# Small reorderings in a four-layer convolution and attention kernel: the samples and the end of layer 0, one weight sum of the MLP, and five places in layers 1 to 3

## The chip, the cores and the metric

The kernel runs on one core of a Trainium2 chip. The metric is the device time in microseconds (us) of one execution, lower is better. The profile comes from one execution, and its times count from the first instruction of that execution.

## What is computed

The reference applies four layers, one after the other, to x of shape (2, 512, 32, 32), that is two batches of 512 channels and 1024 pixels. All values are float32.

```python
# layer 0: attention with sampled keys and a learned bias over positions
q = gconv1x1(bn(x), qw)                        # 8 groups of 64 channels
off = tanh(pw @ gelu(dwconv6x6_stride4(q)))*4  # 64 offsets for each group
kv = grid_sample(bn(x), grid + off)            # bilinear samples
k, v = gconv1x1(kv, kw), gconv1x1(kv, vw)
pos = grid_q - grid_kv                         # 1024 x 64 pairs for each group
bias = relu(relu(sign(pos)*log1p(|pos|) @ w1 + b1) @ w2 + b2) @ w3 + b3
x = x + out_w @ softmax(q k / 8 + bias) v + out_b
x = x + w2 @ gelu(w1 @ bn(x) + b1) + b2        # the MLP, 512 -> 2048 -> 512
# layer 1: group norm, 8-head attention, projection, residual
# layer 2: group norm, 1-head attention, projection, residual
# layer 3: q, k of 64 channels, softmax over axis 1, gamma * (v attn) + x
```

## The kernel before

**Layer 0.** The two batches and four pairs of groups make eight units, t = 0 to 7. A loop over i = 0 to 255 works on 32 steps for each unit. In every step `second` (L623) makes four bias tiles: the matmuls of L630 fill a two-bank PSUM tile z, and ACT evicts it with a Relu (L639). Tiles z come from a pool of three PSUM tiles, and everything else in layer 0 that needs PSUM (`zt`) takes its tile from the same pool. DVE makes the inputs (L613) and joins the four results in two steps (L644). The rest of the unit's work is a chain of generators, `behind`: `finish(t)`, then `offsets(t + 2)`, then `samples(t + 1)`. After every second z tile, one `next(behind)` runs the chain to its next `yield`, and what it emits stands behind that z tile in each engine's queue. Such a place is called a slot here: eight slots make four steps. At the first and the third tile of each step with i % 4 == 1, `scale_tab` (L601) puts one more activation of 128x512 on ACT. Counted from the first slot of a step with i % 4 == 0 as slot 0, these two stand in the gaps after slots 1 and 2 of every eight.

`samples(t)` broadcasts two coordinates into a PSUM tile `gpb` (L504), then makes `near` for two axes with two activations each (L512, L513) in one slot. In the following slots it makes `wx` and the eight planes of `wy` from `gpb` (L519, L520, L523; two planes in the first slot, then three and three), a Relu over all of `wy` (L526), and then the products and copies of keys and values.

Joined tiles are added up over partitions by DMAs with an add, which POOL's queue issues (L970 and its neighbours). The sum of step i - 1 is added to it at step i by L970. For the last step it is a DVE add (L988). The result is summed by `third` (L659) into PSUM tile `sim`, of two banks, and `scores` (L667) adds the query-key product.

`finish_last` (L731) ends the last unit. For each half of 512 columns it issues `third`, `scores` and an ACT copy into `simb` (L743). Then come eight transposes (L753), the row maxima (L754), 16 exponentials with their sums (L761), a division (L770), transposes back (L775), a copy (L776) and the output projection (L719), which DVE adds to x (L729). The pieces `project_out(pps[0], b, 0, [2])` and `project_out(pps[1], b, 1, range(2))` don't depend on the softmax. They stand between the two sets of transposes.

**MLP.** Products use seven multiplications for a 2x2 block product (Strassen's way with sums of Winograd). In block 0, `form2` makes sums of the second weight on DVE: four adds of 128x1024 (L161) for each half of the columns. One add is taken for each chunk c from 4 on by L1353, and the rest after the loop. DVE also forms `upper` (L1306 to L1309) and the right-hand sums of `hid` (L173 to L176).

**Layers 1 to 3.** Every engine keeps the order that the program writes. Eight PSUM banks rotate under one tag. `group` (L1463) does a seven-product group: with K of two chunks its order is x0, y5, v4, z3, x1, y6, v2. Product y6 accumulates on y, so it waits until DVE has read y for u2 (L1494). DVE then makes u3 (L1506), and `evict` combines the rest. Small work stands in tracks with written costs and waits, and `do_chores` takes from them three times in each group, and twice in each turn of `attend`.

- `group_norm` (L1212) yields between its parts. `over_group` multiplies by a matrix of group means (L1224), yields, and then copies the PSUM result on DVE (L1227). Four Newton turns (L1247 to L1249) follow with no yield between.
- `divide` (L1687) sums the exponentials of a head pair with ones, inverts them, and sends them through DRAM to be broadcast: for each part the write to `d` (L1715), then the read into `r` (L1719). Both are on SP's queue. `scale` (L1722) multiplies `o` by `r` on DVE.
- `Weights.total` (L1927) does the same in layers 2 and 3. In layer 2 its sum is over one tile `acc`, two matmuls of 512 columns (L1934) in two column groups, with two DMAs to `few2`.
- `weighed` (L1984) with `evict_last` (L1989) ends layer 3: DVE adds up the last four blocks and stores them (L2133).

Of the kernel before, what the change touches and what calls it, by code (L numbers as in the profile page):

```python
# [12 lines left out]
F32 = mybir.dt.float32  # L13
# [66 lines left out]
def kernel(ctx: ExitStack, tc: tile.TileContext, a: dict, out: bass.AP):  # L80
# [111 lines left out]
    def layer0(l0, fold_d, t2_b, o2_b):  # L192
# [301 lines left out]
        def samples(t):  # L494
            b, pr = divmod(t, NPAIR)
            xt = one.tile([P, 8, P], F32, name="xt", tag="pixels")
            nc.sync.dma_start(
                out=xt, in_=a["xt"][b, :, pr * P : (pr + 1) * P].rearrange("(k p) c -> p k c", p=P)
            )

            gp = gps.pop(t)
            gpb = zt([P, 2, P], "gpb")
            for ax in range(2):
                nc.tensor.matmul(  # L504
                    gpb[:, ax, :], gp[:, ax : ax + 1].to_broadcast([P, P]), ident, start=True, stop=True
                )
            yield

            near = two.tile([P, 2, 32], F32, name="near")
            wsum = two.tile([P, 3], F32, name="wsum")  # L510
            for ax in range(2):
                nc.scalar.activation(near[:, ax, :], ir, AF.Abs, bias=gp[:, ax : ax + 1], scale=-1.0)  # L512
                nc.scalar.activation(  # L513
                    near[:, ax, :], near[:, ax, :], AF.Relu, bias=1.0, scale=-1.0, accum_out=wsum[:, ax : ax + 1]
                )
            nc.vector.tensor_mul(wsum[:, 2:3], wsum[:, 0:1], wsum[:, 1:2])
            yield
            wx = one.tile([P, P], F32, name="wx", tag="values")
            nc.scalar.activation(wx, gpb[:, 0, :], AF.Abs, bias=cs("px"))  # L519
            nc.scalar.activation(wx, wx, AF.Relu, bias=1.0, scale=-1.0)  # L520
            wy = one.tile([P, 8, P], F32, name="wy", tag="wy")
            for k in range(8):
                nc.scalar.activation(wy[:, k, :], gpb[:, 1, :], AF.Abs, bias=cs("py", k))  # L523
                if k % 3 == 1:
                    yield
            nc.scalar.activation(wy, wy, AF.Relu, bias=1.0, scale=-1.0)  # L526
            yield
            nc.vector.tensor_tensor(wy, wy, wx.unsqueeze(1).to_broadcast([P, 8, P]), ALU.mult)
            yield
            yield  # L530

            pk = zt([P, 2, P], "pk")
            accumulate(pk[:, 0, :], [(xt[:, k, :], wy[:, k, :]) for k in range(8)])
            accumulate(pk[:, 1, :], [(wsum[:, 2:3].to_broadcast([P, P]), ident)])
            ow = one.tile([P, C], F32, name="ow", tag="pixels")
            nc.sync.dma_start(out=ow, in_=a["out_w"][pr * P : (pr + 1) * P, :])
# [24 lines left out]
            nc.tensor.matmul(pvo[:, :C], values, ow, start=True, stop=True)  # L561
            vos[t] = vop.tile([P, C], F32, name="vo")
            nc.scalar.copy(vos[t], pvo[:, :C])
            simbias[t] = two.tile([P, 1], F32, name="simbias")
            nc.vector.tensor_add(simbias[t], pb, col("cpb_b3"))
# [165 lines left out]
        def finish_last(sim, eights, fours, right_sums, left_sums):  # L731
# [5 lines left out]
            pps = [zt([P, HW], "pp")]  # L737
            project_out(pps[0], b, 0, range(2))
            simb = one.tile([P, HW], F32, name="simb", tag="wy")
            for half, n in enumerate(halves):  # L740
                third(sim, NR - 8, eights, fours, [half])
                scores(t, sim, [half])
                nc.scalar.activation(simb[:, n], sim[:, n], AF.Identity, bias=simbias[t])  # L743
            ptvs = [pt.rearrange("p i (g j) -> p (i g) j", j=NJ) for pt in pts]
            mx = two.tile([P, 16], F32, name="mx")
# [8 lines left out]
                nc.vector.tensor_reduce(mx[:, g], ptvs[half], AX.X, ALU.max, negate=True)  # L754
            right_sums()
            pps.append(ps_s.tile([P, HW], F32, name="pp", tag="sim"))
            project_out(pps[0], b, 0, [2])
            project_out(pps[1], b, 1, range(2))
            for half, n in enumerate(halves):
                for g in range(half * 8, half * 8 + 8):  # L760
# [167 lines left out]
        for i in range(steps):  # L928
            for k, part in enumerate((1, 0, 3, 2)):
# [37 lines left out]
                        nc.sync.dma_start(out=whole[j:P:4], in_=own[0:P:4])  # L967
                if k == 1 and i - 1 in parts:
                    other = joined(parts.pop(i - 1), 2)
                    nc.gpsimd.dma_start(out=joins[i - 1], in_=other, accum_op=ALU.add)  # L970
                j = (i - 3) % 4
                if k == 1 and 0 <= i - 3 < LAST and j:
                    nc.gpsimd.dma_start(  # L973
# [222 lines left out]
    def layers(f, fold_d, t2_b, o2_b, left1, right1):  # L1196
# [15 lines left out]
        def group_norm(x, gname, bname, h, small_psum):  # L1212
# [9 lines left out]
            def over_group(v, name):  # L1222
                pg = small_psum("pg")[:, :CC]
                nc.tensor.matmul(pg, cs("gmean"), v, start=True, stop=True)  # L1224
                yield
                g = small.tile([P, CC], F32, name=name)
                nc.vector.tensor_copy(g, pg)  # L1227
                return g

            mean = small.tile([P, CC], F32, name="mean")  # L1230
# [12 lines left out]
            nc.vector.tensor_scalar(  # L1243
                rs.bitcast(mybir.dt.int32), var.bitcast(mybir.dt.int32), -0.5, float(0x5F3759DF), ALU.mult, ALU.add
            )
            for _ in range(4):
                nc.vector.tensor_mul(square, rs, rs)  # L1247
                nc.vector.scalar_tensor_tensor(square, square, -0.5, var, ALU.mult, ALU.mult)
                nc.vector.scalar_tensor_tensor(rs, square, 1.5, rs, ALU.add, ALU.mult)  # L1249
            sc = small.tile([P, CC], F32, name="sc")  # L1250
            sh = small.tile([P, CC], F32, name="sh")
            nc.vector.tensor_mul(sc, rs, col(gname, 0, CC))
# [21 lines left out]
        with ExitStack() as mlp:  # L1274
# [57 lines left out]
            for blk in range(NBLK):  # L1332
# [9 lines left out]
                for c in range(MC + 1):  # L1342
# [6 lines left out]
                        upper = combined(pms, p1, hid[:, MC + c, :].rearrange("p (j n) -> p j n", j=2))  # L1349
                    if c:  # L1350
                        form_right2(slice(c - 1, c))
                    if blk == 0 and c >= 4:
                        advance(later[0])  # L1353
                    if b == 1 and c % 2:
                        advance(norm)
# [104 lines left out]
        def seven_right(b11, b12, b21, b22, t1, t2, t4, t3=None):  # L1460
            return b11, b21, b22, t4, t1, t2, b12 if t3 is None else t3

        def group(name, nk, n, stationary, moving, evict, slack, plain=False):  # L1463

            third = nk * n / 256

# [34 lines left out]
                add(z, 3, 3)  # L1501
            add(x, 1, 1, False)
            do_chores(third, slack)
            add(y, 6, 6, False)
            u3 = temp("u3", n)
            nc.vector.tensor_tensor(u3, y, p1, ALU.add)  # L1506
# [31 lines left out]

        def statistics(steps, wait):
            t = track()  # L1540
            for i in range(CC + 5):
                t.append((1.5 if i < CC else 0.5, lambda: advance(steps)))
                if i >= CC:
                    t.append(wait)
# [142 lines left out]
        def divide(o, acc):  # L1687
# [20 lines left out]
            def invert():  # L1708
# [1 line left out]
                note(few)  # L1710
                d, r = sums_d.tile([2, HW], F32, name="d"), unit("r")
                held.append(r)
                for part in range(2):
                    i = slice(part * 64, part * 64 + 64)
                    nc.sync.dma_start(  # L1715
                        out=d[part].rearrange("(h q n) -> q h n", h=2, q=64),
                        in_=few[i].rearrange("q (h n) -> q h n", h=2),
                    )
                    nc.sync.dma_start(out=r[i], in_=d[part].partition_broadcast(64))  # L1719

            def scale():
# [173 lines left out]
        class Weights:  # L1895
# [31 lines left out]
            def total(self):  # L1927
                den, row = bank("den"), temp("row", HALF)
                some = [p.rearrange(self.order, k=2, q=2) for p in (self.p if self.shares else self.acc)]
                n = self.n = min(4, 2 * len(some))  # L1930
                self.few = small.tile([P, 4, HALF // P], F32, name="few2")
                for i in range(2 * len(some)):
                    j = i % n
                    nc.tensor.matmul(  # L1934
# [3 lines left out]
                        start=i < n,  # L1938
                        stop=i + n >= 2 * len(some),
                    )  # L1940
                nc.scalar.copy(row[: 32 * n], den[: 32 * n])
                for i in range(n):
                    nc.sync.dma_start(
                        out=self.few[:, i], in_=row[32 * i : 32 * i + 1].rearrange("o (q n) -> o q n", q=P)
# [39 lines left out]
        def weighed(name, x, qb, seven_sv, w, bias, done=None, last=False):  # L1984

            n = slice(qb * HALF, (qb + 1) * HALF)
            for g in range(2):

                def evict_last(c11, c12, c21, c22):  # L1989
                    for (base, more), i, q in ((c11, 0, 0), (c21, 1, 0), (c22, 1, 1), (c12, 0, 1)):  # L1990
                        m, at = g + 2 * i, qb * HALF + q * QUARTER
                        dst = x[:, m, at : at + QUARTER]
                        if more is not None:
                            nc.vector.tensor_add(dst, dst, more)
                        nc.vector.scalar_tensor_tensor(dst, base, bias[:, m : m + 1], dst, ALU.add, ALU.add)
                        if q:
                            done(m, n)

                def evict(c11, c12, c21, c22):
                    c = unit("c").rearrange("p (m q n) -> p m q n", m=2, q=2)  # L2000
# [14 lines left out]

                group(
                    name, 4, QUARTER, lambda i, s: seven_sv(i, s)[:, g * P : (g + 1) * P], w.seven,
                    evict_last if last and g else evict, 2.6,
                )
                yield  # L2020

# [286 lines left out]
```

## Time and profile before

| | value |
|---|---|
| median of three runs | 3342.02 us (3341.78 to 3342.47) |
| profiled execution, its own time | 3342.55 us |
| its span, first to last instruction | 3340.7 us, so 1.85 us lie around it |
| PE busy | 3316.0 us (99%), 24789 matmul instructions |
| DVE, ACT, POOL busy | 2642.5 us (79%), 1812.4 us (54%), 675.3 us (20%) |
| chain that ended last | PE 96%, DVE 1%, ACT 1%, issue 1% |
| mean granted clock of TensorE | 0.999 |

A float32 matmul stands as two instructions in the records. One instruction of 512 columns starts 0.43 us after the one before, one of 256 columns 0.215 us, one of 128 columns 0.107 us. Its shown duration is some 0.17 us longer[...]. A wait of PE is therefore best read as the distance between two starts, less the normal distance. The timeline gives the idle time in brackets, with what ended it.

### The profile page before, as it was taken

The page shows a single profiled execution, that of the slowest core. Times are in us where ns is not written, and L with a number is a line of the kernel's source. Part 1 is how long each engine was busy: PE and PEld are TensorE (multiplying, and loading weights), DVE is VectorE, ACT ScalarE, POOL GpSimd, SP SyncE. Part 2 cuts the span into 40 slices and gives each one's busy share as a digit, 9 for nine tenths or more (in the row PEclk, how much of TensorE's full clock was granted, in tenths as well). Part 3 has the DMA queues.
Part 4 walks back from the last instruction along what each step waited for, and adds up shares of the span by engine and source line. Part 5 has one row for each costly group of instructions (what it writes and reads, how often), then busy time and mean ns, then how long its engine had stood idle before and what let it go on. Part 6 is the DMA issues. An engine that isn't in the chain of part 4 may idle for free.

```text
span 3340.7 us, 60894 instructions
## 1 busy us (share of the span) xinstructions
PE 3316.0 (99%) x24789; PEld 1600.6 (48%) x24789; DVE 2642.5 (79%) x3033; ACT 1812.4 (54%) x2763; POOL 675.3 (20%) x806
## 2 busy tenths in 40 slices
PE   9999999999999999999999999999999999999999
PEld 4333333333333333333333339999953443687777
DVE  7999999999998899999999966455446465665556
ACT  4866877877876677877867642112136245122221
POOL 1333333333333233333333210000000000000000
PEclk9999999999999999999999999999999999999999
DMA  5887787787777587787787741000100000000111
GB/s 178 165 167 150 158 167 159 156 168 154 161 161 157 109 168 152 163 163 158 162 165 155 154 119 58 14 11 11 52 0 14 26 33 16 7 7 4 29 33 36
DMA packets 142993, 343.92 MB, mean 103 GB/s; under 512 B 36976, under 2 KB 51952, under 8 KB 141936
## 3 DMA queue, kind: packets, MB, share of 16 engines
q0 software_dynamic: 68400, 231.26, 37.1%
q1 hardware_dynamic: 71056, 102.12, 10.2%
q10 hardware_dynamic: 3248, 6.56, 0.5%
q8 instruction: 197, 3.23, 0.4%
q14 instruction: 92, 0.75, 0.1%
HBM read 71.46 MB, written 10.83 MB: 25 GB/s over the span
## 4 chain that ended last, share of the span: by engine, by line
PE 96%; DVE 1%; issue 1%; ACT 1%; DMA 0%; ACTq 0%; POOL 0%; DVEq 0%; POOLq 0%
PE z L630 52%; PE pma L135 6%; PE pw L1471 6%; PE pmb L135 5%; PE pmv L1471 4%; PE score L1650 3%; PE pv L1662 3%; PE pm L1471 3%; PE score L1471 3%; PE pmt L1471 1%; PE ppr L1471 1%; PE sim L659 1%; PE pf L135 1%; PE pp L719 1%; PE pma L1374 1%
## 5 line engine op out<-in xcount | busy, mean ns | idle before, releaser
L630 PE MATMUL z<-wa,cpb_w 128*32 128x512 f32 x10880 | 1192.2, 593 | 3.4 <-ACT h L639 3.4
L639 ACT ACTIVATE h<-z,b2h 128x1024 f32<-128x1024 f32 x768 | 852.1, 1115 | 329.2 <-PE z L630 300.4
L613 DVE CUSTOM_DVE_ANT_1 wa<-tab,pairs 128x2048 f32<-128x2048 f32 x340 | 779.9, 2295 | 2.9 <-PE z L630 2.5
L630 PEld LDWEIGHTS z<-wa,cpb_w 128*32 128x32 f32 x10880 | 346.2, 110 | 809.7 <-issue 713.6
L630 PE MATMUL z<-h,cpb_w 128*32 128x512 f32 x5504 | 609.4, 593 | 0.7 <-ACT h L639 0.7
L613 DVE CUSTOM_DVE_ANT_1 h<-tab,pairs 128x2048 f32<-128x2048 f32 x172 | 394.7, 2295 | 1.3 <-PE z L630 1.0
L630 PEld LDWEIGHTS z<-h,cpb_w 128*32 128x32 f32 x5504 | 175.6, 110 | 407.9 <-issue 364.3
L644 DVE SCALAR_TENSOR_TENSOR h<-h,turn,h 128x1024 f32<-128x1024 f32 x256 | 329.8, 1288 | 5.5 <-ACT h L639 5.5
L639 ACT ACTIVATE bridge<-z,b2h 128x1024 f32<-128x1024 f32 x162 | 181.1, 1118 | 118.6 <-PE z L630 118.6
L963 POOL DMA_DIRECT2D bridge<-bridge x150 | 127.6, 850 | 530.6 <-DMA bridge<-h 498.1
L644 DVE SCALAR_TENSOR_TENSOR bridge<-bridge,turn,h 128x1024 f32<-128x1024 f32 x162 | 208.3, 1286 | 5.2 <-ACT bridge L639 5.2
L970 POOL DMA_DIRECT2D bridge<-h x161 | 151.7, 942 | 289.3 <-DVE h L644 175.1
L1314 ACT COPY p<-pma 128x128 f32<-128x128 f32 x80 | 21.4, 267 | 334.4 <-PE pma L135 313.3
L1306 DVE TENSOR_TENSOR upper<-pma,p 128x256 f32<-128x256 f32 x80 | 33.8, 422 | 178.5 <-ACT p L1314 178.4
L1651 ACT ACTIVATE p<-score 128x512 f32<-128x512 f32 x256 | 130.3, 628 | 81.0 <-PE score L1650 79.9
L963 POOL DMA_DIRECT2D h2j<-h2j x90 | 76.2, 847 | 313.0 <-DMA h2j<-h 304.2
L639 ACT ACTIVATE h2j<-z,b2h 128x1024 f32<-128x1024 f32 x94 | 105.1, 1118 | 41.8 <-PE z L630 41.2
L1683 DVE TENSOR_TENSOR acc<-acc,p 128x1024 f32<-128x1024 f32 x96 | 111.2, 1219 | 19.8 <-ACT p L1651 19.5
L1650 PE MATMUL score<-q,k 64*128 64x512 f32 x512 | 120.7, 604 | 1.1 <-DVE gm L1227 1.1
L644 DVE SCALAR_TENSOR_TENSOR h2j<-h2j,turn,h 128x1024 f32<-128x1024 f32 x94 | 121.3, 1290 | 0.0
L1662 PE MATMUL pv<-p,vT 128*64 128x512 f32 x512 | 116.5, 598 | 0.0
L973 POOL DMA_DIRECT2D bridge<-bridge x90 | 108.4, 1204 | 3.2 <-DMA bridge<-bridge 2.5
(463 smaller groups left out, 4369.5 us busy)
## 6 DMA issues: line engine op xcount, KB each, us to landing
bridge<-h POOLq DMA_DIRECT2D x161, 512.0 KB, 5.2
h2j<-h POOLq DMA_DIRECT2D x94, 512.0 KB, 5.5
bridge<-bridge POOLq DMA_DIRECT2D x159, 256.0 KB, 3.6
tab<-slog_d SPq DMA_DIRECT2D x128, 256.0 KB, 5.0
h2j<-h2j POOLq DMA_DIRECT2D x90, 256.0 KB, 3.2
bridge<-bridge POOLq DMA_DIRECT2D x150, 128.0 KB, 5.2
bridge<-bridge SPq DMA_DIRECT2D x90, 128.0 KB, 3.9
bridge<-h2j SPq DMA_DIRECT2D x90, 128.0 KB, 3.7
```

Source lines behind the costliest of these rows:

```text
L135: nc.tensor.matmul(pm, w, m, start=(k == 0), stop=(k == len(pairs) - 1))
L613: nc.vector._custom_dve(TENSOR_ADD_SAT, out=h1, in0=tx.unsqueeze(1).to_broadcast([P, H, 2, W]), in1=ty.unsqueeze(3).to_broadcast([P, H, 2, ...
L630: nc.tensor.matmul(z[point * 32 : point * 32 + 32, n], cpb_w2[:, lo : lo + 32], h1s[point][:, half * 16 : half * 16 + 16, :], start=True, ...
L639: nc.scalar.activation(h2, z, AF.Relu, bias=b2h[:, part : part + 1])
L644: nc.vector.scalar_tensor_tensor(h2, h2, turn[:, part // 2 : part // 2 + 1], parts.pop(part + 1), ALU.mult, ALU.add)
L963: nc.gpsimd.dma_start(out=own[0:P:2], in_=own[1:P:2], accum_op=ALU.add)
L970: nc.gpsimd.dma_start(out=joins[i - 1], in_=other, accum_op=ALU.add)
L1471: nc.tensor.matmul(out, stationary(l, k), moving(r, k), start=start and k == 0, stop=k == nk - 1, skip_group_check=not start,)
L1650: nc.tensor.matmul(sc, ks[m][r, s * P : (s + 1) * P], qs[m][r, n], start=True, stop=True)
L1651: nc.scalar.activation(p[:, part], sc, AF.Exp, scale=64 ** -0.5)
L1662: nc.tensor.matmul(pv[half][part * 64 : part * 64 + 64], vt[s % 4][:, lo : lo + 64], lps[s, half][:, part, :], start=(s == 0), stop=(s == 7),)
L1683: nc.vector.tensor_add(acc[half], acc[half], ps[s, half])
```

## The change

There are nine edits. The listing is cut to its core.

1. `samples`: a `yield` between the two axes of `near`. All that follows in the chain of that unit comes one slot later.
2. `finish_last`: both halves of `third` and `scores` first, then `project_out(pps[0], b, 0, [2])`, and then both ACT copies.
3. The layer-0 loop: for i = 254 and 255 the add of L970 is done by DVE.
4. MLP, block 0: no weight sum is taken at c = 7 and 8.
5. `over_group`: the copy is on ACT, ahead of the yield.
6. `group_norm`: a yield after two Newton turns, with one more step in `statistics`.
7. `divide`: both writes to `d` ahead of both reads into `r`.
8. `Weights.total` in layer 2: four matmuls of 256 columns in four column groups, one ACT copy of 128x256, four DMAs into 64 partitions each.
9. `group` and `weighed`: for the last group of all, `early` adds base, bias, u2 and x for all four blocks after product x1, and stores the first block. `evict_last` adds what is left and stores each of the other three blocks as it is done.

```diff
@@ samples
                 nc.scalar.activation(
                     near[:, ax, :], near[:, ax, :], AF.Relu, bias=1.0, scale=-1.0, accum_out=wsum[:, ax : ax + 1]
                 )
+                if ax == 0:
+                    yield
@@ finish_last
-            for half, n in enumerate(halves):
+            for half in range(2):
                 third(sim, NR - 8, eights, fours, [half])
                 scores(t, sim, [half])
+            project_out(pps[0], b, 0, [2])
+            for n in halves:
                 nc.scalar.activation(simb[:, n], sim[:, n], AF.Identity, bias=simbias[t])
...
             pps.append(ps_s.tile([P, HW], F32, name="pp", tag="sim"))
-            project_out(pps[0], b, 0, [2])
             project_out(pps[1], b, 1, range(2))
@@ the loop of layer 0
-                    nc.gpsimd.dma_start(out=joins[i - 1], in_=other, accum_op=ALU.add)
+                    if i < steps - 2:
+                        nc.gpsimd.dma_start(out=joins[i - 1], in_=other, accum_op=ALU.add)
+                    else:
+                        nc.vector.tensor_add(joins[i - 1], joins[i - 1], other)
@@ over_group
+                g = small.tile([P, CC], F32, name=name)
+                nc.scalar.copy(g, pg)
                 yield
-                g = small.tile([P, CC], F32, name=name)
-                nc.vector.tensor_copy(g, pg)
@@ group_norm
-            for _ in range(4):
+            for turn in range(4):
...
+                if turn == 1:
+                    yield
@@ MLP
-                    if blk == 0 and c >= 4:
+                    if blk == 0 and 4 <= c < MC - 1:
                         advance(later[0])
@@ group
             add(x, 1, 1, False)
             do_chores(third, slack)
+            if early is not None:
+                early(x, u2, z, p5)
             add(y, 6, 6, False)
@@ statistics
-            for i in range(CC + 5):
+            for i in range(CC + 6):
@@ divide
-                for part in range(2):
-                    i = slice(part * 64, part * 64 + 64)
+                halves = [slice(part * 64, part * 64 + 64) for part in range(2)]
+                for part, i in enumerate(halves):
                     nc.sync.dma_start(
                        out=d[part].rearrange("(h q n) -> q h n", h=2, q=64),
                        in_=few[i].rearrange("q (h n) -> q h n", h=2),
                    )
+                for part, i in enumerate(halves):
                     nc.sync.dma_start(out=r[i], in_=d[part].partition_broadcast(64))
@@ Weights.total
+                if not self.shares:
+                    self.n = 2
+                    quarters = [(k, q) for k in range(2) for q in range(2)]
+                    for i, (k, q) in enumerate(quarters):
+                        nc.tensor.matmul(
+                            den[32 * i : 32 * i + 32, :QUARTER], ones[:, :32], some[0][:, k, q], start=True, stop=True
+                        )
+                    nc.scalar.copy(row[:, :QUARTER], den[:, :QUARTER])
+                    for i, (k, q) in enumerate(quarters):
+                        nc.sync.dma_start(
+                            out=self.few[64 * q : 64 * q + 64, k],
+                            in_=row[32 * i : 32 * i + 1, :QUARTER].rearrange("o (p n) -> o p n", p=64),
+                        )
+                    return
@@ weighed
+                def early(c11, u2, c21, c22):
+                    for base, i, q in ((c11, 0, 0), (c21, 1, 0), (c22, 1, 1), (u2, 0, 1)):
+                        m, at = block(i, q)
+                        nc.vector.scalar_tensor_tensor(
+                            x[:, m, at], base, bias[:, m : m + 1], x[:, m, at], ALU.add, ALU.add
+                        )
+                    done(*block(0, 0))
+
                 def evict_last(c11, c12, c21, c22):
-                    for (base, more), i, q in ((c11, 0, 0), (c21, 1, 0), (c22, 1, 1), (c12, 0, 1)):
...
+                    for more, i, q in ((c21[1], 1, 0), (c22[1], 1, 1), (c12[0], 0, 1)):
+                        m, at = block(i, q)
+                        nc.vector.tensor_add(x[:, m, at], x[:, m, at], more)
+                        done(m, at)
```

More of the change, by code (lines that the diff above doesn't have):

```diff
@@ L1461, in seven_right, with group @@
             return b11, b21, b22, t4, t1, t2, b12 if t3 is None else t3
-        def group(name, nk, n, stationary, moving, evict, slack, plain=False):
+        def group(name, nk, n, stationary, moving, evict, slack, plain=False, early=None):
             third = nk * n / 256
@@ L1929, in total @@
                 some = [p.rearrange(self.order, k=2, q=2) for p in (self.p if self.shares else self.acc)]
-                n = self.n = min(4, 2 * len(some))
                 self.few = small.tile([P, 4, HALF // P], F32, name="few2")
+                if not self.shares:
[12 more added lines that the diff above has]
+                    return
+                n = self.n = 4
                 for i in range(2 * len(some)):
@@ L1940, in total @@
                     )
-                nc.scalar.copy(row[: 32 * n], den[: 32 * n])
+                nc.scalar.copy(row, den)
                 for i in range(n):
@@ L1987, in weighed, with block @@
             for g in range(2):
-                def evict_last(c11, c12, c21, c22):
-                    for (base, more), i, q in ((c11, 0, 0), (c21, 1, 0), (c22, 1, 1), (c12, 0, 1)):
[L1991 to L1997, printed above, removed]
+                def block(i, q):
+                    at = qb * HALF + q * QUARTER
+                    return g + 2 * i, slice(at, at + QUARTER)
+                def early(c11, u2, c21, c22):
[5 more added lines that the diff above has]
+                    done(*block(0, 0))
+                def evict_last(c11, c12, c21, c22):
+                    for more, i, q in ((c21[1], 1, 0), (c22[1], 1, 1), (c12[0], 0, 1)):
+                        m, at = block(i, q)
+                        nc.vector.tensor_add(x[:, m, at], x[:, m, at], more)
+                        done(m, at)
                 def evict(c11, c12, c21, c22):
@@ L2017, in weighed @@
                     name, 4, QUARTER, lambda i, s: seven_sv(i, s)[:, g * P : (g + 1) * P], w.seven,
-                    evict_last if last and g else evict, 2.6,
+                    evict_last if last and g else evict, 2.6, early=early if last and g else None,
                 )
```

## The prediction

> **What bounds the kernel now.** I read the page's busy line first, then the waits of PE in order of size, then timelines around each wait. The busy line and the chain say that the end waits for PE nearly always.
>
> ```profile
> PE 3316.0 (99%) x24789; PEld 1600.6 (48%) x24789; DVE 2642.5 (79%) x3033; ACT 1812.4 (54%) x2763; POOL 675.3 (20%) x806
> ```
>
> So a time is won only where PE stands, or where it does less. The waits of PE (total, times, longest) are a short list:
>
> ```profile
> PE z L630 <- ACT h L639: 4.1, 6, 0.7
> ...
> PE sim L659 <- DMA bridge<-h: 2.1, 1, 2.1
> PE pmv L1471 <- DVE u L1494: 1.7, 2, 1.3
> PE score L1650 <- DVE gm L1227: 1.1, 1, 1.1
> PE pma L1374 <- ACT hid L1339: 0.9, 1, 0.9
> PE pma L135 <- POOL ones L1328: 0.9, 1, 0.9
> PE sim L659 <- ACT simb L743: 0.8, 1, 0.8
> ```
>
> Every edit but three (den, Newton and the tail) points at a line of this list; Newton's is the one below it, score L1471 with 0.7. From start to start a wait is some 0.17 us longer than listed. Each of the six L630 waits is thus 0.84. PE's timeline at the end of layer 0 shows more than its waits:
>
> ```profile
> 1968.37 1.06 PE L659 MATMUL sim<-bridge,w 128*32 128x512 f32 x6
> 1971.51 0.62 PE L659 MATMUL sim<-bridge,w 128*32 128x512 f32 x1 [2.09 <-DMA bridge<-h]
> ...
> 1973.77 2.07 PE L667 MATMUL sim<-x,kqs 128*128 128x512 f32 x2
> 1976.62 1.06 PE L659 MATMUL sim<-bridge,w 128*32 128x512 f32 x8 [0.78 <-ACT simb L743]
> ```
>
> L667 takes 2.07 for the first half, 1.13 for the second. The window from 1972.90 to 1976.20 has a granted clock of 0.50, the windows before and after it 1.00: the idle stretch is paid twice.
>
> [...] the step into den (L1934) costs 0.09 extra, and four column groups of z start within 0.02. [...] On SP's queue the trace has 1.8 to 3.3 for d<-few and 2.1 for most stores.
>
> **The change, part by part.** Sums are against the profiled span, 3340.7, which has 1.85 around it (3342.55, own time). That run lies 0.5 above the median 3342.02, so a saving is taken off the median.
>
> *Samples (edit 1).* ACT at one of the six places:
>
> ```profile
> 443.85 0.31 ACT L512 ACTIVATE near<-ir,gp 128x32 f32<-128x32 f32 x1
> ...
> 445.00 0.82 ACT L601 ACTIVATE pairs<-tab,pc 128x512 f32<-128x512 f32 x1
> 445.73 2.10 ACT L639 ACTIVATE h<-z,b2h 128x1024 f32<-128x1024 f32 x2
> ```
>
> From 443.85 to 445.73 is 1.88 of other work ahead of the z eviction, and PE waits 0.84. Where `near` comes without `pairs` (1195.34 to 1196.49, 1.15) PE waits 0.11. Both say that a burst of 1.04 is free while `gpb` holds one of the three PSUM tiles, and that the excess is the wait. After the edit the same slot has half of near (0.58, from 443.85 to 444.43) and pairs (0.73), so 1.31: 0.27 is left. The second half, 0.58, is free. `wx` with its first two planes (1.13) is now one slot further from the wait that shielded it: 0.09. So 0.84 becomes 0.36 or so, 0.47 won six times, 2.8. Two of the eight units have another phase. In samples(4) three planes of wy (0.75) now meet tab (0.71) with gpb still held: 1.46, 0.42 lost, less the 0.09 shift that goes before; with wx that is 0.4 against 0.11 now. In samples(7) nothing changes by more than 0.1. The later products and copies have spare slots: they end at slot 46 of 64. **Sum 2.5**; 1.0 if wy costs more, 3.5 if wx is free.
>
> *End of layer 0 (edits 2, 3).* The DVE adds replace POOL DMAs whose second one, issued at 1960.99 amid the load of mlp_w, landed at 1971.47. Each add is 1.23 (row L988). DVE idles 2.15 before each of its last joins, so both fit, and nobody on DVE or POOL is later. `third` then goes through from 1968.37: four rounds of 0.43 where the broken sequence took six, at full clock. With scores (1.06) and the switches the first half is over at 1971.2, the second, no longer behind ACT, at 1974.1. The moved piece of pp, four instructions or 1.7, lasts to 1975.8. ACT's two copies (0.69 each) end at about 1975.6 even if the first waits for both halves of sim, so both sets of transposes go without a wait, to 1976.7. Next are eight pp instructions, 3.43, to 1980.1. The softmax on ACT and DVE takes 4.54 from the last transpose of half 0 (1979.77 to 1984.31 before), and the second half 6.93. PE, having spent 1.7 of its cover, now waits 0.6 and then 0.25 there. The transposes back end at 1983.5 instead of 1988.6: **5.1**. It is 3.5 if the halves of sim or the clock hold PE longer, 6.0 if no new wait arises. What follows (pp, L729, L161) moves as a block.
>
> *MLP (edit 4).* The add that holds PE's chunk 7 back is the one at c = 6 (2032.60, ahead of L1306 at 2033.95), which stays. The one at c = 7 (2036.32) goes behind the right-hand sums, and its result is needed by the last of six products, at 2045.76. **0**; at most 0.3 either way. If the cover of those products were gone, it would cost its 1.22.
>
> *Copy on ACT (edit 5).* PE waited 1.27 from start to start at 2732.90 for a bank that DVE freed 9.4 after its matmul (2723.14). ACT reaches the copy after four exponentials, at 2724.45, 0.9 after the matmul, so the bank is free long before. The copy is some 0.2 (nearest row: th<-po, 128x2, 0.16), in ACT's idle 3.43 of that turn. Behind it stand the next exponentials, for which PE's pv has a turn's room. **1.3**, ends 0.9 and 1.3.
>
> *Newton (edit 6).* At 2924.67 PE waits 0.85 for u2, which stood behind a burst of 18 tiny DVE operations (3.4, from 2915.79) and the sums after it. The split moves nine of them (1.8). With a wait of 3.0 in the track they come two calls of do_chores later, still ahead of that u2. Meanwhile the work between waits for PE once, so I get u2 at 2924.15 where PE wants it at 2923.78. **0.4**, ends 0 and 0.85.
>
> *divide (edit 7).* SP's timeline:
>
> ```profile
> 2842.83 0.63 SPq L1715 DMA_DIRECT2D d<-few  x1
> 2846.22 0.46 SPq L1719 DMA_DIRECT2D r<-d  x1
> 2846.76 0.63 SPq L1715 DMA_DIRECT2D d<-few  x1
> 2850.01 0.46 SPq L1719 DMA_DIRECT2D r<-d  x1
> ```
>
> The second write stands behind a read that waits for the first, and `scale` on DVE starts only when the second read has landed, 2853.61, after 2.05 idle. With both writes first, the second read is issued near 2847 and lands near 2851 (3.6, the median of r<-d). DVE is free at 2851.55, so its backlog begins 2.0 sooner. Behind it stand two u2 that PE waits for, 0.64 and 1.43. The first goes. For the second PE arrives 0.64 sooner and DVE 1.95 sooner, leaving 0.1. **2.0**, ends 0.6 and 2.1. The other divides hide: PE shows no wait there.
>
> *den (edit 8).* PE does two instructions of 512 columns one after the other in two column groups; now two rounds of 256 in four. From 2929.18 to 2930.16 is 0.98; it becomes 0.55. Four times 0.43: **1.7**, at least 1.3. Two more DMAs of about 0.6 land at 2969.6 instead of 2968.3 in the tightest place, where DVE reads them at 2970.9; without that cover it would be 1.3 late.
>
> *Tail (edit 9).* After PE's last matmul (it ends at 3333.24) DVE still does three operations in a row; the last two are:
>
> ```profile
> 3334.05 0.42 DVE L1994 TENSOR_TENSOR x<-x,u 128x256 f32<-128x256 f32 x1
> 3334.58 0.48 DVE L1995 SCALAR_TENSOR_TENSOR x<-pw,gb,x 128x256 f32<-128x256 f32 x1
> ```
>
> They end at 3335.06. After the edit the four `early` adds lie between 3329.8 (x1 done) and 3331.5, in front of u3, which could not start before 3331.55 anyway. Two adds of 0.42 follow, and the last waits for PE (3333.24) and ends at 3333.72: 1.34 sooner. The store is half as long, and its own time was 3.3 against 2.1 elsewhere, so I add 0.4. **1.7**, ends 0.9 and 2.5.
>
> Sum: 2.5 + 5.1 + 0 + 1.3 + 0.4 + 2.0 + 1.7 + 1.7 = 14.7. The span goes to 3326.0, the median to **3327.3**. The lows sum to 8.2, the highs to 18.0.
>
> **The rivals.** *The waits move.* DVE is 79% busy and ran without a gap from 2915.45 to 2929.46. If layer 2's backlog keeps its u2 late (edits 6 and 7 give 0.5), softmax at the end of layer 0 takes back 2 and the samples give 1, then 9.2: 3332.8. For it: three of the eight savings assume that DVE arrives as I shifted it. Against: the divide's idle time is a plain DMA wait. Half its gain again gone is the same case, up to 3335.3.
>
> *It does little.* Taken that sim's halves serialise on a whole-tile rule also for ACT's read, that r<-d is slowed by its twin to 7, and that the wy planes hit tab and pairs in every unit (16 bursts of 1.46, each 0.42): 14.7 less 2.0, 2.0 and 6.7 leaves 4.0: 3338.0. Against the last: only units 4 and 7 have that phase. That an edit doesn't act at all is so for the MLP's, in my count.
>
> *Slower.* ACT's copy now stands ahead of the work that PE waits for. If PE reaches the matmul of group means later than ACT reaches the copy, ACT's whole queue waits, and PE for it. Six of the eight copies lie in attention or scores; a turn is 7.2. To end at the old time each must cost 14.7 / 6 = 2.5; at a full half turn, 3.6 each or 21.6, the kernel ends at 3348.9. It decides from ACT arriving over 2.5 ahead of PE. For it: in the scores group margins are thin (matmul at 2911.51, ACT free at 2911.10). Against: there ACT waits 0.4 at most.
>
> **How the numbers follow.** My sum: 0.66. The waits move: 0.21. Little: 0.08. Slower: 0.05. The first two are faster by over 0.2% (6.7 us, about what a measurement of this kernel can tell from no change). Faster 0.87, same 0.08, slower 0.05. The likeliest case spans 3324.0 to 3333.8 by the bounds; all ends at once are unlikely, and the second case lies at its upper edge, so the range is 3323.3 to 3333.0.
>
> **What would show it.** The waits of PE lose sim<-DMA, sim<-simb and gm. L630's six fall to 0.1 or 0.2 each, with one new one near 1207. The clock stays at 1.00 in the 1970s. New waits for at (L775) of 0.6 and 0.25 appear. The pma L1374 wait stays near 0.9. Den takes 0.55. DVE's last operation ends 0.5 after PE. A 2924-like wait of 0.85, or a DVE still idle before L1722, would make me wrong there; an ACT gap ended by pg would speak for the slower case.

## The result and the profile after

The changed kernel takes 3326.63 us (median of five runs, 3326.56 to 3327.36) against 3341.78 before (3340.88 to 3342.47). The ratio is 0.9956, 95% interval 0.9946 to 0.9967. The profiled execution has a span of 3324.8. By the unrounded ends of the two traces (3340.75 and 3324.77) that is 16.0 less than before; 14.7 had been worked out. The medians differ by 15.2. PE is busy for less time and stands for less:

```profile
PE 3311.0 (100%) x24805; PEld 1599.6 (48%) x24805; DVE 2643.8 (80%) x3027; ACT 1809.0 (54%) x2771; POOL 672.8 (20%) x804
```

The waits of PE after; those of the first 31 us are left out at the marks. Of the list of before only the two pma waits are left in their old size, z has shrunk to what is shown, and at is new:

```profile
...
PE pma L1382 <- ACT hid L1347: 0.9, 1, 0.9
PE pma L135 <- POOL ones L1336: 0.9, 1, 0.9
...
PE pt L778 <- DVE at L773: 0.5, 1, 0.5
...
PE z L632 <- ACT h L641: 0.2, 1, 0.2
```

The wait list has a lower limit; from start to start the six z waits stand at 0.26 each, and a seventh, at 1206.70, at 0.34.

PE's timeline at the end of layer 0:

```profile
1968.03 1.13 PE L669 MATMUL sim<-x,kqs 128*128 128x512 f32 x2
1969.09 1.07 PE L661 MATMUL sim<-bridge,w 128*32 128x512 f32 x8
...
1970.94 1.13 PE L669 MATMUL sim<-x,kqs 128*128 128x512 f32 x2
1971.90 1.88 PE L721 MATMUL pp<-aT,vo 128*128 128x512 f32 x4
...
1978.62 0.63 PE L778 MATMUL pt<-cst,at 128*128 128x128 f32 x4 [0.53 <-DVE at L773]
```

L661 of the second half goes in unbroken rounds, both L669 take 1.13, and the only listed gap is the one for at. ACT at the sample that was shown of before:

```profile
444.17 0.83 ACT L603 ACTIVATE pairs<-tab,pc 128x512 f32<-128x512 f32 x1
444.90 2.26 ACT L641 ACTIVATE h<-z,b2h 128x1024 f32<-128x1024 f32 x2
```

`near` of one axis starts at 443.60 ahead of these two, so 1.30 of other work lies before the eviction, where it was 1.88. SP at the last divide, and DVE's last operations:

```profile
2833.41 1.35 SPq L1725 DMA_DIRECT2D d<-few  x2
2835.31 1.82 SPq L1730 DMA_DIRECT2D r<-d  x2
```

```profile
3318.00 0.76 DVE L2029 TENSOR_TENSOR x<-x,u 128x256 f32<-128x256 f32 x2
3319.27 0.42 DVE L2029 TENSOR_TENSOR x<-x,pw 128x256 f32<-128x256 f32 x1 [0.51 <-PE pw L1479]
```

**Where the 16.0 came from.** The same PE instruction was found in both traces, and its start in one taken from its start in the other. What this shift grows by at an edit is the edit's gain. It is one execution against one, so what varies between executions at that very place is still in it; this matters for the divide and for the tail. Edit 1 was not undone by itself, and edits 4 and 9, and 5 and 8, were undone in pairs and read apart by their places.

| step | foretold | between the traces | in a run with it undone |
|---|---|---|---|
| start, first 20 us (no edit) | 0 | -0.2 | |
| samples (1) | 2.5 | 2.41 | |
| end of layer 0 (2, 3) | 5.1 | 4.98 | 0.45 and 4.8 |
| MLP (4) | 0 | 0.00 | 0.0 |
| copy on ACT (5) | 1.3 | 2.22 | 2.25 |
| Newton (6) | 0.4 | 0.78 | 0.62 |
| divide (7) | 2.0 | 2.15 | 0.67 or 1.48 |
| den (8) | 1.7 | 1.65 | 1.65 |
| tail (9) | 1.7 | 1.97 | 1.91 |
| sum | 14.7 | 16.0 | |

### The profile page after: what moved, and what is told of

Read it like the earlier page. It is cut to its first block, busy times and chain, and to the rows that moved or that the text cites. A ratio compares the mean times of both kernels' runs of the same rounds, so it can differ in the third digit from the quotient of the medians.

```text
span 3324.8 us, 60957 instructions
## 1 busy us (share of the span) xinstructions
PE 3311.0 (100%) x24805; PEld 1599.6 (48%) x24805; DVE 2643.8 (80%) x3027; ACT 1809.0 (54%) x2771; POOL 672.8 (20%) x804
## 4 chain that ended last, share of the span: by engine, by line
PE 97%; issue 1%; ACT 1%; DVE 1%; POOL 0%; ACTq 0%; DVEq 0%; POOLq 0%
PE z L632 53%; PE pw L1479 6%; PE pma L135 6%; PE pmb L135 5%; PE pmv L1479 4%; PE score L1660 4%; PE pv L1672 3%; PE pm L1479 3%; PE score L1479 3%; PE pmt L1479 1%; PE ppr L1479 1%; PE pp L721 1%; PE sim L661 1%; PE pf L135 1%; PE pma L1382 1%
```

## Experiments

All start from the changed kernel. "Loss" and "gain" are growths of the shift against it at the place concerned; times are medians. Three of the runs (with edit 3, with edit 6, and with edits 4 and 9 undone) begin 1.6 to 1.9 late in their profiled execution for a reason in the first 20 us that no edit touches (last section), so spans are not compared. The medians carry this too: with edits 4 and 9 undone the five executions took 3328.4, 3328.4, 3329.7, 3330.4 and 3330.6. A median can therefore differ from a reading in the traces by up to 2.

**The end of layer 0, edit 3 undone.**

```diff
-                    if i < steps - 2:
-                        nc.gpsimd.dma_start(out=joins[i - 1], in_=other, accum_op=ALU.add)
-                    else:
-                        nc.vector.tensor_add(joins[i - 1], joins[i - 1], other)
+                    nc.gpsimd.dma_start(out=joins[i - 1], in_=other, accum_op=ALU.add)
```

> The changed kernel with edit 3 undone: the sums for i = 254 and 255 are POOL DMAs again, the new order of finish_last stays. My theory: the DMA lands near 1969.2, PE waits for it some 2.2 inside third, the four column groups fall apart (0.9), and the clock is halved for 3.4 (some 1.7 of work lost), none of which the new order can hide, since PE has nothing else queued. Loss 4.0 to 5.0, so 3330.6 to 3331.6, and the clock near 0.5 in a window of the 1970s. Rival, the order is the main part of the 5.0 and the DMA wait only its bare length: loss 2.2, 3328.8, clock 1.00. A second rival, the DMA is quicker than before because less is in flight: loss under 1.

Measured: 3330.54. The loss is 4.8, as the first theory has it. PE's timeline, and a window over the stretch after the wait (the column after the engines is PE's granted clock):

```profile
1967.92 1.06 PE L661 MATMUL sim<-bridge,w 128*32 128x512 f32 x6
1971.09 1.06 PE L661 MATMUL sim<-bridge,w 128*32 128x512 f32 x1 [2.12 <-DMA bridge<-h]
```

```profile
1971.10:1974.40 3.30, 3.30 (x6) 0.53 (x6) 0.00 (x0) 0.00 (x0) 0.00 (x0) 0.50 0.44 184
```

The twelve instructions of this half should go in four rounds (four, four, two and two). Six go in two rounds, and the next start 3.17 after the first. What is left takes four more rounds, two of pairs and two of single instructions, 0.86 apart, and each lasts 1.06 instead of 0.59: the clock is 0.50. A wait of 2.28, two rounds more at 0.43, and four rounds that take 0.86 instead of 0.43 come to 4.9. So 2.28 of waiting costs 4.8. The order alone, edit 2, hides nothing of it.

**Edit 2 undone**: each half is copied right after its scores, and `project_out(pps[0], b, 0, [2])` goes back behind the transposes.

```diff
-            for half in range(2):
+            for half, n in enumerate(halves):
                 third(sim, NR - 8, eights, fours, [half])
                 scores(t, sim, [half])
-            project_out(pps[0], b, 0, [2])
-            for n in halves:
                 nc.scalar.activation(simb[:, n], sim[:, n], AF.Identity, bias=simbias[t])
...
+            project_out(pps[0], b, 0, [2])
             project_out(pps[1], b, 1, range(2))
```

> The changed kernel with edit 2 undone: each half of sim is copied by ACT right after its scores, the moved piece of pp is back behind the transposes; the DVE adds stay. My theory: the waits for simb return (1.2 to 1.4 before the second third, 0.5 before the transposes), the wait for at of 0.69 goes, since the twelve pp instructions cover it again; no DMA wait, clock 1.00. Loss 1.0 to 1.3, so 3327.6 to 3327.9. Rival, the waits for simb were drawn out by the halved clock and by the broken column groups: then each is under 0.8 and the loss under 0.5. Other rival, an idle stretch of 1.4 halves the clock by itself: loss 2.5 or more and a clock near 0.5.

Measured: 3327.27, a loss of 0.45. My theory was too high. The first rival has the loss right (under 0.5), though not the length of the first wait (under 0.8):

```profile
1970.00 1.07 PE L661 MATMUL sim<-bridge,w 128*32 128x512 f32 x8 [0.78 <-ACT simb L745]
...
1973.76 0.66 PE L755 MATMUL pt<-cst,simb 128*128 128x128 f32 x4 [0.34 <-ACT simb L745]
```

From start to start the two waits are 0.94 and 0.51, and the first was 1.41 before. The instruction ahead of it ran at a clock of 0.50 there (the window of before, up to 1976.20); 0.43 more for it is most of the difference of 0.47. Against the two stands the at wait, 0.69, which is gone here, since twelve pp instructions cover the softmax. So nearly the whole 4.98 is the DVE adds: 4.5 by this run, 4.8 by the other. The order is worth 0.2 to 0.45.

**The transposes, pp piece cut in two** (new).

```diff
-            project_out(pps[0], b, 0, [2])
+            project_out(pps[0], b, 0, [2], [0])
...
                 nc.vector.tensor_reduce(mx[:, g], ptvs[half], AX.X, ALU.max, negate=True)
+                if half == 0:
+                    project_out(pps[0], b, 0, [2], [1])
             right_sums()
```

> The changed kernel with the moved piece of pp cut in two: two of its four instructions before the transposes of the first half of simb, two behind them. My theory (PE waits 0.69 for at because its cover of eight pp instructions is shorter than the softmax): the softmax of the first half starts 0.86 sooner, the wait goes, the second set of transposes waits under 0.1; gain 0.5 to 0.7, 3326.0. Rival, ACT's exponentials and not the start set it, since ACT's copy of the second half stands before them: the wait stays above 0.5.

Measured: 3325.25, gain 0.69. No wait for at is left, as its transposes follow the eight pp instructions at once:

```profile
1974.21 3.60 PE L721 MATMUL pp<-aT,vo 128*128 128x512 f32 x8
1977.64 0.60 PE L780 MATMUL pt<-cst,at 128*128 128x128 f32 x4
```

The wait was the length of the softmax behind its start, as the prediction took it.

**The samples, near in other slots** (new).

```diff
             yield
+            if t not in (4, NT - 1):
+                yield

             near = two.tile([P, 2, 32], F32, name="near")
...
-                if ax == 0:
+                if ax == 0 and t != 4:
                     yield
```

> The changed kernel with one more yield ahead of near in all units but 4 and 7, and none between its two axes in unit 4. My theory (a burst of ACT work over 1.04 between two z evictions, while gpb holds a PSUM tile, is PE's wait): the slot with pairs now has no near, so the six waits of 0.26 go, and in unit 4 the planes of wy leave the slots with tab and pairs, so 0.34 falls to 0.11. Gain 1.6 to 1.9, 3324.8. Rival, the wait is of gpb's longer hold as such, by whatever stands behind it: one slot later the waits stay or grow, 3326.6 to 3327.5.

Measured: 3325.52, gain 1.68. The six waits and the one of unit 4 fall below 0.2; in unit 0 a new one of 0.35 appears, at 190.38, for DVE's write of kvbd, now one slot later. So the waits of z are the ACT work in one gap, and moving it to a free gap takes them away. ACT at the same sample now has `pairs` alone ahead of the eviction, 0.74:

```profile
443.63 0.84 ACT L605 ACTIVATE pairs<-tab,pc 128x512 f32<-128x512 f32 x1
444.37 1.11 ACT L643 ACTIVATE h<-z,b2h 128x1024 f32<-128x1024 f32 x1
```

**The MLP and the tail, edits 4 and 9 undone.** The condition is `c >= 4` again, and `evict_last` is that of before.

> The changed kernel with edits 4 and 9 undone: the MLP's weight sum at c = 7 and 8 is back, and the last group ends as before. My theory: PE's starts through the MLP stay where they are to within 0.1, the wait of 1.08 near 2029 stays; the tail, from PE's last start to the end of the span, is 1.9 longer; 3328.5. Rival for the MLP, the add costs its own 1.22: 3329.7. Rival for the tail, the last store and not the DVE chain sets the end, and it takes what it took (3.3): only 0.9 longer, 3327.5.

Measured: 3329.68. Through the MLP the shift moves by less than 0.05, so edit 4 does nothing. From PE's last start to the end of the span it is 1.91 longer, so the rival for the tail (0.9) is out.

**The MLP, one chunk less** (new).

```diff
-                    if blk == 0 and 4 <= c < MC - 1:
+                    if blk == 0 and 4 <= c < MC - 2:
```

> The changed kernel with the MLP's weight sums stopped one chunk sooner (4 <= c < MC - 2). My theory, from the prediction: the add at c = 6 is what holds back hid of the last chunk; without it DVE is there 1.22 sooner, and the wait of 1.08 near 2029 goes or falls under 0.2, with the four adds left hidden behind the last products; gain 0.9 to 1.1, 3325.6. Rival, the wait is the plain length of the chain from the product through DVE's combination and ACT's gelu to hid: it stays at 0.8 or more, 3326.6. Other rival, the sums get late behind the loop and PE waits for them near 2040: no gain or a loss up to 1.2.

Measured: 3325.38, gain 1.17. The pma wait (1.08 from start to start) is gone, and none comes later. The add at c = 6 did hold the last chunk back.

**The copy and den, edits 5 and 8 undone.** The copy is on DVE behind the yield; den is two groups of 512 columns.

> The changed kernel with edits 5 and 8 undone, which lie 190 us apart and are read apart in the trace. Copy on DVE: the trace of before shows after the wait at 2732.90 two score instructions that run alone in their row group, and two that ran alone ahead of it, so my theory after the result is that the wait of 1.27 costs two more rounds of 0.43 because the two heads' halves no longer run together: PE falls back by 2.1 to 2.3 there. Rival, my prediction's figure, the wait alone: 1.3. den: PE falls back by 0.41 at each of four places, 1.65 in sum; rival, four column groups don't run at once and it costs nothing. Time by my theory 3330.5, by the first rival 3329.6, without den 3328.8.

Measured: 3331.07. The copy costs 2.25, den 4 x 0.41. In the changed kernel a den takes 0.57 from its start to the next product's, where it took 0.98:

```profile
2916.83 0.64 PE L1946 MATMUL den<-acc,ones 128*32 128x256 f32 x8
2917.40 1.13 PE L1479 MATMUL score<-t,h2t 128*128 128x256 f32 x4
```

How a wait of 1.26 costs 2.25 can be counted from the score matmuls, which run as pairs, one in each half of the rows. First before, then the changed kernel:

```profile
2728.96 2.84 PE L1650 MATMUL score<-q,k 64*128 64x512 f32 x10
2732.90 1.98 PE L1650 MATMUL score<-q,k 64*128 64x512 f32 x6 [1.11 <-DVE gm L1227]
```

```profile
2721.76 3.70 PE L1660 MATMUL score<-q,k 64*128 64x512 f32 x16
```

Sixteen instructions are eight rounds of 0.43. Before, the single records show four rounds paired (2728.96 to 2730.35), two of one head alone (2730.78, 2731.21), the wait, two paired, and two of the other head alone (2733.87, 2734.30): ten rounds. 1.27 + 2 x 0.43 is 2.1; the first step behind the wait is 0.53 instead of 0.43, another 0.1. The records don't name the heads; my reading, from the order of the program, is that the two heads take turns, the first head's product has its bank and goes alone, the second head's waits for a bank, and all that follows waits behind it. It then runs beside the first head of the next pair, whose own partner is left alone at the end. In the run with edits 5 and 8 undone a wait of 0.27 stands at 2915.54, for u. That is Newton's place with the split in and the copy on DVE.

**Newton, edit 6 undone**: no yield at `turn == 1`, and `CC + 5` steps.

> The changed kernel with edit 6 undone: four Newton turns without a yield between. My theory: near 2912 PE waits again for u, 0.6 to 0.8 from start to start (the ACT copy has taken 0.15 from DVE's burst), so 3327.3, at the limit of what the time can show; the trace shows it. Rival, the divide's order and not the split removed that wait: no wait there, 3326.6.

Measured: 3327.50; the wait for u is back, 0.66 from start to start, and the loss is 0.62.

```profile
PE score L1477 <- DVE u L1500: 0.5, 1, 0.5
```

**Divide, edit 7 undone**: each read right behind its own write.

> The changed kernel with edit 7 undone: each read into r directly behind its own write to d. My theory: DVE idles 2 before scale, the waits for u near 2845 and 2853 come back with 0.64 and 1.43, sum 2.1, and the one near 2912 does not; 3328.7. Rival, part of the two waits came from DVE's backlog behind the group norms, which the split and the ACT copy have thinned: only 0.6 to 1.0 comes back, 3327.2 to 3327.6. Other rival, the late divide pushes its backlog on to the Newton place: 0.8 more, 3329.5.

Measured: 3327.10. Only one wait, of 0.70, and a loss of 0.67. My theory was wrong. But the rival's reason, a thinner backlog, is not it either: DVE's operations ahead of `scale` are the same, and DVE idles 0.58 before it instead of 2.05, because the first write to d took 1.85 and not the 3.33 of the profiled execution before. DVE at `scale`, before and in this run:

```profile
2853.61 1.23 DVE L1722 TENSOR_TENSOR o<-o,r 128x1024 f32<-128x1024 f32 x1 [2.05 <-DMA r<-d]
```

```profile
2842.64 1.23 DVE L1732 TENSOR_TENSOR o<-o,r 128x1024 f32<-128x1024 f32 x1 [0.58 <-DMA r<-d]
```

A window from that write on, of before:

```profile
DMA  0000000000090001420000000010000000000000
...
q8 instruction: 1, 0.02, 2.3%
```

One fetch of instructions, 16 KB, starts at 2843.75, ahead of the write's 144 packets. In the records it lasts to 2845.08, and nine of the packets start only then, 0.7 after the others. The records don't name the DMA engine; that the nine stood behind the fetch is read from these times. With edit 7 undone, no fetch lies beside that write. One more run tests whether the write sets the loss.

**Divide paired, where the write had been slow**: edit 7 undone in the kernel with one MLP chunk less, whose write took 2.9.

> The run with the MLP's sums stopped a chunk sooner, with edit 7 undone. In that run the first write to d of the last divide took 2.9, as it took 3.3 before and 1.85 elsewhere; a fetch of instructions of 16 KB lies beside each slow one. My theory: what edit 7 is worth depends on that write. If it is slow again (2.9), DVE idles some 1.65 before scale and PE waits for the two u by 1.6 to 1.8 in sum; if it is quick (1.85), 0.70. Rival, the write has nothing to do with it and DVE's backlog decides: 0.7 with a slow write. Time 3326.9 or 3326.0.

```profile
2832.69 0.63 SPq L1725 DMA_DIRECT2D d<-few  x1
2835.82 0.46 SPq L1729 DMA_DIRECT2D r<-d  x1
```

```profile
2842.80 1.23 DVE L1732 TENSOR_TENSOR o<-o,r 128x1024 f32<-128x1024 f32 x1 [1.38 <-DMA r<-d]
```

Measured: 3328.86. As the two lines of SP show, the read came 3.13 after the write. The write took 3.08 with a fetch beside it; the loss is 1.48, with the wait for u at 1.43. So it was a little under the 1.6 foretold, and far over the 0.7 of a quick write. The three cases agree: DVE idles 0.58, 1.38 and 2.05 before `scale`, and 0.67, 1.48 and 2.15 is lost, 0.1 more each time. What edit 7 is worth here goes with the first write: it took 3.33 before and 3.08 in this run, in which a 16 KB fetch started 0.9 to 1.0 after it, and 1.85 with edit 7 undone, in which none lay beside it. The median of this run is 3.5 above that of the kernel with one MLP chunk less, though. Its profiled execution was the fastest of four (3327.22); what the other three paid is not shown. With edit 7 in, slow writes (3.1 as the median of the two in the run with copy and den undone, 2.9 for the first in the one with one MLP chunk less) left no wait behind.

**All three new edits together**, `near` moved in units 1 to 3, 5 and 6.

> The changed kernel with near one slot later (units 1 to 3, 5, 6), none between its axes in unit 4, the MLP's sums stopped one chunk sooner and the pp piece cut in two. If the three gains add: samples 1.6, MLP 1.2, transposes 0.7, so 3.5 below the changed kernel, 3323.1. Rival, what is won ahead of the transposes or of the MLP is taken back there: 3324.5 or more.

Measured: 3322.77; to the kernel before the ratio is 0.9942, interval 0.9928 to 0.9955. The gains add: 3.6 at the end, from samples 1.77, transposes 0.72 and MLP 1.17. Of PE's waits behind the start, the largest left is pma at L135 (1.05), which no edit here touches.

## Why the prediction was right, and where its terms were off

- **The frame.** Every gain but the tail's was a wait of PE or less work for PE, and the only new wait of PE for DVE was the one foretold, for at. "The waits move", "little" and "slower" are out. The sum fell 1.3 short of 16.0, and 1.3 of that is the copy (0.92) and Newton (0.38); the other terms were off by up to 0.3 each, which nearly cancels with the start. At the last divide the twin reads took 3.5 and 4.0, not 7, and only unit 4 met the wy planes. Of the eight copies of pg on ACT, seven came 1.0 to 1.2 after their matmul, and the eighth (2900.25) made ACT wait 0.7, far from 2.5, with nobody on PE waiting for it.
- **Samples.** 0.47 was foretold for each of six places and 0.45 measured, with the 0.26 and the 0.1 for wx (0.08 at 453.05) where they were put. Unit 4 lost 0.35, against 0.29. The burst of 1.30 left 0.26, so 1.04 was free again, and with `near` moved neither `near` nor `pairs` made a burst over 1.04.
- **End of layer 0.** The four stages ended within 0.1 of the worked times, the at wait was 0.69 against 0.6, the second one 0.18 against 0.25. What the sum didn't say is that it hangs almost wholly on edit 3.
- **MLP.** 0, for the reason given; the run with one chunk less bears it out.
- **Copy, mis-sized: 1.3 against 2.22.** The wait was taken at its length. The same text counted broken rounds for the column groups of `third`, and the score's row pairs should have been looked at in the same way.
- **Newton, mis-sized: 0.4 against 0.78.** The residue of 0.37 is there (0.27) when the copy is on DVE. Edit 5 takes that copy out of the same burst, and the sum priced the two apart.
- **Divide.** 2.0 against 2.15, yet the size rests in part on a fetch: 1.48 of the 2.05 idle came from the slow first write. The text took 3.3 as the upper end of an ordinary spread. So the close hit is in part luck: forecast and measurement rest on the same execution of before, and against one with a quick write the gain is 0.67.
- **den and tail.** den: 0.41 against 0.43 each. Tail: DVE's last operation ended 1.36 sooner after PE's last start, against 1.34. The 0.4 for a store of half the size is not shown: the last store, of 128 KB, took 3.22 to land, against 3.33 for 256 KB before, and with edits 4 and 9 undone the last two, of 256 KB each, have a median of 3.2. The 0.6 that came off beside DVE's share is, against the kernel before, 0.11 of that store and 0.49 between its landing and the end of the span, where SP ends its last waits (2.33 and then 1.84). That the size came near is in part luck.

## What to carry to other kernels

A wait inside matmuls that run side by side in groups can cost more than it lasts (2.28 cost 4.8 and 1.27 cost 2.2 here, while the waits of z cost no more than their length): look at the rounds on both sides of it, and at the clock behind it, before you price its end. Price edits that touch the same burst of small operations together. Of a DMA that took longer than its twins in the trace, find out what was beside it before you count on the difference.

## What was not expected of the hardware

- The clock was 0.50 for 3.41 (1972.87 to 1976.28) behind the wait of 2.25 before, and 0.50 from 1971.10 to 1974.40 behind that of 2.28 with edit 3 undone. It was 1.00 behind the waits of 1.27 (2732.90) and 1.43 (2862.80) before, and behind that of 1.43 in the last run with edit 7 undone; with edit 2 undone, where one of 0.94 stands, its mean over the run is 1.000. In the clock records, full clock lasts 1966.08 from 6.79 on before, then half clock 3.41 and full clock 1361.92; in the changed kernel it lasts 3317.76 from 5.58 on. These are 576, 1, 399 and 972 times 3.4133. Taken in such steps from 6.79 on, PE's records of before leave 2.06 idle in the step ahead of the halved one, and 1.55 at most in any other that holds a product. Whether the idle time of one step decides is not shown.
- In three profiled executions the start took 1.6 to 1.9 longer. In each of them the clock was 0.66 from 15 to 20; before, in the changed kernel and in the last run with edit 7 undone it was 1.00 there. With edit 3 undone, the six instructions of pwarm took 5.49 against 4.46 in the changed kernel, and tw at 15.99 was 0.58 late; at 1967.92 PE was 1.75 late, so 1.2 came behind 15.99. The idle time ahead of it doesn't tell the two apart: from 10 to 15, PE was idle for 1.21 there and for 1.16 in the changed kernel. Why the clock fell is open.
- A fetch of 16 KB of instructions lasted 1.33 at the last divide of before, and the write of 4 KB issued 0.92 ahead of it landed after 3.33; the first writes of the other seven divides took 1.84 to 1.87. Of the sixteen writes in the changed kernel's divides, one took 3.41, issued 1.36 ahead of a fetch that lasted 0.90, and the others 1.83 to 1.87. Fetches that began 1.62 and 1.69 after a write, one in each trace, left it at 1.84.
- In each of the eight divides of before, the write issued behind a read on SP's queue landed after 2.97 to 3.28, beside a fetch of 16 KB in two of them (3.14 and 3.18); the one ahead of the read took 1.84 to 1.87 in seven.
